# The last tile of a graph layer in four column groups, and the ends of its last two tiles between the next layer's first steps

## The chip, the cores and the metric

The kernel runs on one core of a Trainium2 chip. A time is the device time of one execution in microseconds (us). Three runs of the kernel before gave 1924.24, 1925.73 and 1928.12 us, with a median of 1925.73 us. One further execution was profiled, and all views of the profile come from that one.

## What is computed

Four graph layers, each with a residual and a layer norm, over N = 2708 nodes with F = 256 features and a dense float32 adjacency matrix `adj`. The change touches layer 0 and the beginning of layer 1:

```python
# layer 0
x = layernorm(x + adj @ (x * W))
# layer 1: graph attention, 4 heads of 64
h = (x @ W1).reshape(n, 4, 64)
src, dst = einsum('nhd,d->nh', h, a[:64]), einsum('nhd,d->nh', h, a[64:])
e = leaky_relu(src[:, :, None] + dst.T[None, :, :], 0.2)
attn = softmax(where(adj[:, None, :] > 0, e, -9e15), axis=-1)
out = layernorm(einsum('nhm,mhd->nhd', attn, h)) * gamma + beta
x = layernorm(x + out)
# layers 2 and 3 follow; they read adj again
```

## The kernel before

The nodes are cut into NT = 22 tiles of 128 rows; the last one has 2708 - 21 * 128 = 20 rows. `xs[t]` holds the features of tile t and is overwritten layer by layer. `turn` is one wide tile of 22 * 257 columns; `x0e[t]` is its part for tile t, the input features with a column of ones beside them, so that one matmul gives both the aggregate and the row sum of `adj`. Later layers use `turn` again, for blocks of `adj` and for intermediate rows.

**Layer 0** takes a strip of `adj` for each tile (`load_strip`, on SP's queue, two buffers). `strip_matmul` (line 202) sums over 22 chunks: stationary is the chunk's part of the strip (128 by the tile's rows), moving is `x0e[c]` (257 columns). A float32 matmul appears in the trace as two passes, each with its weight load, so a tile has 44. From the same strip `layer0_mask` makes the tile's columns of `mask` on DVE, and `layer0_own` the diagonal on DVE and a test for negative values on ACT. The end of a tile is `layer0_scale` (row sum and product with `w0_b`, reading PSUM) and `layer0_rest`: add the input (line 467), layer norm (bn_stats, bn_aggr, an add on DVE, a power on POOL, line 167, and a normalisation, line 173), then `layer1_projection`. That transposes the tile on PE (line 179), copies it on ACT (line 181), multiplies it by the weights of layer 1 (`pm`, line 410), takes three exponentials on ACT (lines 413 to 416: `rise`, the factor in `hs`, and `fall`), multiplies into `hs[t]` on DVE (line 417), transposes `fall` on PE (`pf`, line 424) and stores it to DRAM through POOL's queue (line 427).

**Layer 1** needs for a step c the tile `hs[c]`, its column of `rise`, a row of `fall` loaded back and broadcast (`fall_b`), and `mask`. It runs over three rounds g of up to eight destination tiles, in each over two pairs of heads q, and in each over the 22 steps c. A step makes two `p` on DVE (line 665, 128 by 1024), which live in four buffers, and then eight matmuls: `heads` (line 647; 64-column groups, two side by side) and `totals` (line 656; 32-column groups, four side by side, all into one PSUM bank `den`). Every second step does totals first. After the matmuls of a step, `step(c)` issues one piece of each piece-wise list of work in `steps`: in rounds 1 and 2 the ends of the tiles of the round before (`layer1_end`, whose row result `o` lies in eight buffers of a pool), in round 0 nothing.

[...] The list of an engine is not quite the order of the Python code. The framework that builds the program moves instructions forward where its own estimate lets it, so that for instance the passes of tile t+1 stand around the projection of tile t on PE, and a reciprocal that is needed only in layer 2 (line 836) stands at the end of layer 0 on DVE. Memory of a closed pool is used again by the next one, tile by tile, with waits where a buffer overlays another: layer 1's pool `l1` lies where layer 0's pool `l0` with the strips was.

Of the kernel before, what the change touches and what calls it, by code (L numbers as in the profile page):

```python
# [9 lines left out]
F32 = mybir.dt.float32  # L10
# [5 lines left out]
ALU = mybir.AluOpType  # L16
AX = mybir.AxisListType
PSUM = bass.MemoryType.PSUM

P = 128  # L20
# [7 lines left out]
def kernel(  # L28
# [24 lines left out]
    nc = tc.nc  # L53
    N, F = x.shape
    NT = -(-N // P)
# [6 lines left out]
    W = GT * P  # L62
    CT = 32
# [17 lines left out]
    def sz(i):  # L81
        return min(P, N - i * P)
# [4 lines left out]
    def bcast(row, n):  # L87
        return bass.AP(tensor=row.tensor, offset=row.offset, ap=[[0, P], [1, n]])
# [13 lines left out]
    def pool(name, bufs=1, **kw):  # L102
        return tc.tile_pool(name=name, bufs=bufs, reuse_waits="tile", **kw)
# [55 lines left out]
    def moments(src, n):  # L159

        bst = small.tile([P, 6], F32, tag="bn_st", name="bn_st")
        nc.vector.bn_stats(bst[:n], src[:n])
        mv = small.tile([P, 2], F32, tag="bn_mv", name="bn_mv", bufs=12)
        nc.vector.bn_aggr(mv[:n], bst[:n])
        rstd = small.tile([P, 1], F32, tag="bn_rs", name="bn_rs", bufs=12)
        nc.vector.tensor_scalar(rstd[:n], mv[:n, 1:2], EPS, None, ALU.add)  # L166
        nc.gpsimd.tensor_tensor(rstd[:n], rstd[:n], neg_half[:n], ALU.pow)  # L167
        return mv[:n, 0:1], rstd[:n]

    def layernorm(dst, src, n):  # L170

        mean, rs = moments(src, n)
        nc.vector.tensor_scalar(dst[:n], src[:n], mean, rs, ALU.subtract, ALU.mult)

    def transposed(ps, pool, src, n, tag):

        pt = ps.tile([P, 4, P], F32, tag="tr", name="tr")
        for f in range(FC):
            nc.tensor.transpose(pt[:, f, :n], src[:n, f * P : (f + 1) * P], ident[:n, :n])
        dst = pool.tile([P, FC, P], F32, tag=tag, name=tag)  # L180
        nc.scalar.copy(dst[:, :, :n], pt[:, :FC, :n])
        return dst
# [18 lines left out]
    def strip_matmul(acc, s, n, rhs):  # L201
        for c in range(NT):
            nc.tensor.matmul(acc, s[:, c, :n], rhs(c), start=(c == 0), stop=(c == NT - 1))  # L203
# [181 lines left out]
    if True:  # L385
# [13 lines left out]
        if True:  # L399
# [5 lines left out]
            def layer1_projection(pool, t):  # L405
                n = sz(t)
                xt = transposed(ps_t, pool, xs[t], n, "xt")
                pm = ps_t.tile([P, 4, P], F32, tag="tr", name="pm").rearrange("p i q -> p (i q)")
                for f in range(FC):
                    nc.tensor.matmul(  # L410
                        pm[:n, : F + 2 * H], xt[:, f, :n], w1_a[:, f], start=(f == 0), stop=(f == FC - 1)
                    )
# [3 lines left out]
                nc.scalar.activation(fall[:n], pm[:n, :H], AF.Exp, scale=ALPHA - 1.0)  # L416
                nc.vector.tensor_tensor(
                    hs[t][:n, :, :HD],
                    pm[:n, H : H + F].rearrange("p (h d) -> p h d", d=HD),
                    hs[t][:n, :, HD:].to_broadcast([n, H, HD]),  # L420
                    ALU.mult,
                )
                pf = ps_t.tile([P, 4, P], F32, tag="tr", name="pf")
                nc.tensor.transpose(pf[:H, 0, :n], fall[:n], ident[:n, :n])
                turned = pool.tile([H, P], F32, tag="turned", name="turned")
                nc.scalar.copy(turned[:, :n], pf[:H, 0, :n])
                nc.gpsimd.dma_start(fall_d[:, t * P : t * P + n], turned[:, :n])

                for g in [g for g, (lo, hi) in enumerate(spans[:4]) if hi == t + 1]:
                    load_fall(falls[g // 2], g, nc.gpsimd)  # L430

            with pool("l0", 2) as l0:
                w0_b = l0.tile([P, F], F32, name="w0_b", bufs=1)
                nc.scalar.dma_start(w0_b, bcast(w0, F))

                def layer0_mask(t, s, lo=0, hi=NT):
                    n = sz(t)
# [19 lines left out]
                def layer0_scale(t, acc):  # L457
                    n = sz(t)

                    nc.vector.tensor_scalar(rdeg[:n, t : t + 1], acc[:n, F:FE], 1.0, None, ALU.add)  # L460
                    nc.vector.tensor_tensor(xs[t][:n], acc[:n, :F], w0_b[:n], ALU.mult)

                def layer0_rest(t, acc=None):
                    n = sz(t)
                    if acc is not None:
                        layer0_scale(t, acc)
                    nc.vector.tensor_tensor(xs[t][:n], xs[t][:n], x0[t][:n], ALU.add)
                    layernorm(xs[t], xs[t], n)
                    layer1_projection(l0, t)


                ahead = 3
                with pool("prep", side="right") as prep:
# [45 lines left out]
                    acc = ps_acc.tile([P, 512], F32, tag="acc", name="acc")  # L519
                    strip_matmul(acc[:, :FE], strips[ahead], P, lambda c: x0e[c])  # L520
                    for t in range(ahead):
                        layer0_rest(t)
# [25 lines left out]
                falls = [fallp.tile([P, H, 2 * W], F32, tag="fall_b", name="fall_b") for _ in range(2)]  # L548
                nc.sync.dma_start(gamma_b, bcast(gamma, F))
                nc.sync.dma_start(beta_b, bcast(beta, F))  # L550
                for t in range(ahead + 1, NT):
                    s = load_strip(l0, t)
                    last, acc = acc, ps_acc.tile([P, 512], F32, tag="acc", name="acc")
                    strip_matmul(acc[: sz(t), :FE], s, sz(t), lambda c: x0e[c])
                    layer0_mask(t, s)
                    layer0_own(t, s)

                    layer0_rest(t - 1, last)
                layer0_rest(NT - 1, acc)

            l1 = keep_stack.enter_context(pool("l1", 2))
            if True:

                def layer1_end(pool, t, s, sums, dens):
# [12 lines left out]
                    if s == 0:  # L577
                        nc.vector.reciprocal(rden[:n], totals)
                    else:
                        for q in range(H // 2):  # L580
                            nc.vector.reciprocal(rden[:n, q], totals[:, q ^ s])
                    o = pool.tile([P, F], F32, tag="o", name="o", bufs=len(ended))
                    nc.vector.tensor_tensor(
                        o[:n].rearrange("p (h d) -> p h d", d=HD),
                        pt[:n, : H // 2, :].rearrange("p q (i d) -> p (q i) d", d=HD),
                        rden[:n].rearrange("p q i -> p (q i)")[:, :, None].to_broadcast([n, H, HD]),
                        ALU.mult,
                    )
# [26 lines left out]
                for g in range(0, len(spans), 2):  # L615
# [4 lines left out]
                        for i in range(len(segs)):  # L620
                            load_fall(falls[-1], g + i, nc.sync)
                    cols = [(lo * P - at, width(lo, hi)) for lo, hi in segs]
                    sums, steps, halves = [], [], []

                    def step(c):
                        for s in list(steps):
# [13 lines left out]
                    for q in range(H // 2):  # L640
# [42 lines left out]
                    ended = [(t, s, sums, dens) for s, (lo, hi) in enumerate(segs) for t in range(lo, hi)]  # L683


                acc_stack.close()
# [785 lines left out]
```

## Time and profile before

| what | us |
|---|---|
| median of three runs | 1925.73 (1924.24 to 1928.12) |
| the profiled execution's own time | 1929.04 |
| span from its first to its last instruction | 1927.3 |
| layer 0, to the last pass of the 20-row tile | to 255.2 |
| first matmul of layer 1 | 263.92 |
| last matmul of layer 1 | 629.7 |

Times in the views are microseconds from the start of the span. PE is the matmul engine, PEld its weight loads, DVE, ACT and POOL are the vector, scalar and general engines, SP issues loads. A line of a timeline has the start, the length, the engine, the source line, the operation, what it writes and reads with shapes, how many instructions are merged, and in brackets how long the engine had been idle before it and what ended that wait. [...] In a window, each engine's busy time stands before the number of its instructions in brackets, and the granted clock of PE is 1.00 at full speed.

### The profile page before, as it was taken

How to read it: one execution, taken by the hardware profiler on the slowest of the kernel's cores; microseconds unless marked ns; L12 is line 12 of the kernel's file. 1: busy time of each engine (PE TensorE's matmuls, PEld its weight loads, DVE VectorE, ACT ScalarE, POOL GpSimd, SP SyncE). 2: the span in 40 equal slices, each digit the busy share in tenths (PEclk: the TensorE clock that was granted, in tenths of full speed). 3: DMA queues.
4: the chain of work that ended last, by engine and by line, in shares of the span. 5: the costliest groups of instructions: out<-in, count | busy, mean ns of one | idle time of the engine just before them, and what ended most of it. 6: DMA issues, size and time to landing. Idle time of an engine off the chain costs nothing.

```text
span 1927.3 us, 22585 instructions
## 1 busy us (share of the span) xinstructions
PE 1864.0 (97%) x7475; PEld 1011.5 (52%) x7479; DVE 1316.4 (68%) x2409; ACT 617.2 (32%) x1064; POOL 261.2 (14%) x435
## 2 busy tenths in 40 slices
PE   8999989999999999999899999999999999999996
PEld 7788832222233778678444444444445555654444
DVE  4334368899898947455557889585877758855665
ACT  4444400000100103111355656455555555311001
POOL 1212110001112421000001000020200101211101
PEclk9999999999999999999999999999999999999998
DMA  8334400000000647555746656454554444643653
GB/s 294 123 143 159 155 23 1 2 28 9 15 1 23 157 103 194 141 131 121 206 137 187 182 163 174 121 158 112 148 155 127 116 114 124 186 115 97 197 152 101
DMA packets 432922, 235.90 MB, mean 122 GB/s; under 512 B 172150, under 2 KB 420620, under 8 KB 430364
## 3 DMA queue, kind: packets, MB, share of 16 engines
q1 hardware_dynamic: 416158, 207.40, 39.2%
q0 software_dynamic: 7760, 21.20, 3.5%
q10 hardware_dynamic: 8878, 5.76, 1.0%
q8 instruction: 62, 1.02, 0.2%
q14 instruction: 64, 0.52, 0.1%
HBM read 221.61 MB, written 12.65 MB: 122 GB/s over the span
## 4 chain that ended last, share of the span: by engine, by line
PE 80%; DMA 6%; DVE 6%; ACT 3%; issue 2%; SPq 2%; POOL 1%; ACTq 0%; DVEq 0%; POOLq 0%
PE m L309 38%; PE acc L647 10%; PE acc L203 7%; PE bank L1007 7%; PE den L656 5%; PE gate L882 4%; PE bank L983 3%; DMA strip<-in_adj_t_dram 2%; DVE p L665 2%; PE bank L1058 2%; SPq L256 1%; ACT below L452 1%; DVE p L1141 1%; PE pm L410 1%; POOL bn_rs L167 1%
## 5 line engine op out<-in xcount | busy, mean ns | idle before, releaser
L665 DVE SCALAR_TENSOR_TENSOR p<-fall_b,rise,mask 128x1024 f32<-128x1024 f32 (+1 forms) x264 | 297.7, 1150 | 27.1 <-PE den L656 14.6
L1137 ACT ACTIVATE p<-st,e_neg 128x1024 f32<-128x1024 f32 (+1 forms) x198 | 197.1, 1040 | 207.8 <-PE m L309 195.4
L309 PE MATMUL m<-s,xq 128*128 128x512 f32 (+3 forms) x660 | 230.3, 467 | 0.0
L647 PE MATMUL acc<-p,h 128*64 128x512 f32 (+2 forms) x1056 | 224.0, 556 | 3.0 <-DVE p L665 2.8
L203 PE MATMUL acc<-turn,strip 128*128 128x257 f32 (+1 forms) x836 | 191.6, 380 | 0.0
L309 PE MATMUL m<-p,xq 128*128 128x512 f32 (+1 forms) x396 | 183.9, 546 | 0.3 <-DVE p L297 0.3
L1140 ACT ACTIVATE p<-p 128x1024 f32<-128x1024 f32 (+1 forms) x198 | 178.8, 943 | 0.2
L309 PE MATMUL m<-p,x 128*128 128x512 f32 (+1 forms) x396 | 169.7, 547 | 5.1 <-DVE p L1141 4.8
L1141 DVE TENSOR_TENSOR p<-p,blk 128x1024 f32<-128x1024 f32 (+1 forms) x132 | 142.5, 1098 | 42.3 <-ACT p L1140 29.9
L296 DVE TENSOR_TENSOR s<-p 128x512 f32<-128x512 f32 (+1 forms) x132 | 83.1, 631 | 120.9 <-PE m L309 101.9
L203 PEld LDWEIGHTS acc<-turn,strip 128*128 128x128 f32 (+1 forms) x836 | 151.5, 185 | 25.3 <-issue 0.5
L309 PEld LDWEIGHTS m<-s,xq 128*128 128x128 f32 x660 | 124.7, 191 | 75.2 <-issue 58.9
L647 PEld LDWEIGHTS acc<-p,h 128*64 128x64 f32 x1056 | 65.5, 136 | 147.8 <-issue 117.5
L167 POOL TENSOR_TENSOR bn_rs<-bn_rs,neg_half 128x1 f32<-128x1 f32 (+1 forms) x110 | 81.8, 745 | 380.1 <-DVE bn_rs L166 373.2
L309 PE MATMUL m<-s,x 128*128 128x512 f32 (+3 forms) x330 | 127.2, 467 | 0.0
L656 PE MATMUL den<-p,h 128*32 128x512 f32 (+2 forms) x1056 | 124.1, 551 | 2.8 <-DVE p L665 2.7
L309 PEld LDWEIGHTS m<-p,x 128*128 128x128 f32 x396 | 74.9, 191 | 79.2 <-issue 61.1
L309 PEld LDWEIGHTS m<-p,xq 128*128 128x128 f32 x396 | 74.5, 190 | 77.8 <-issue 61.2
L452 ACT ACTIVATE below<-strip 128x384 bf16<-128x384 f32 x132 | 78.5, 594 | 72.6 <-DMA strip<-in_adj_t_dram 69.2
L1141 DVE TENSOR_TENSOR p<-p,turn 128x1024 f32<-128x1024 f32 (+1 forms) x66 | 71.6, 1107 | 21.4 <-ACT p L1140 13.3
L681 ACT COPY den<-den 64x512 f32<-64x512 f32 (+2 forms) x12 | 6.3, 529 | 249.2 <-PE den L656 249.1
L297 DVE TENSOR_TENSOR p<-p 128x512 f32<-128x512 f32 (+1 forms) x132 | 83.0, 629 | 1.7
(243 smaller groups left out, 2514.9 us busy)
## 6 DMA issues: line engine op xcount, KB each, us to landing
strip<-in_adj_t_dram SPq DMA_DIRECT2D x19, 1408.0 KB, 6.2
blk<-in_adj_t_dram SPq DMA_DIRECT2D x88, 256.0 KB, 3.4
blk<-in_adj_t_dram SPq DMA_DIRECT2D x88, 192.0 KB, 4.0
pa<-in_adj_t_dram SPq DMA_DIRECT2D x110, 128.0 KB, 2.7
turn<-in_adj_t_dram SPq DMA_DIRECT2D x44, 256.0 KB, 3.1
blk<-in_adj_t_dram SPq DMA_DIRECT2D x88, 128.0 KB, 2.5
p<-in_adj_t_dram SPq DMA_DIRECT2D x44, 256.0 KB, 3.5
turn<-in_adj_t_dram SPq DMA_DIRECT2D x44, 192.0 KB, 3.2
```

What stands on the lines that cost most here:

```text
L167: nc.gpsimd.tensor_tensor(rstd[:n], rstd[:n], neg_half[:n], ALU.pow)
L203: nc.tensor.matmul(acc, s[:, c, :n], rhs(c), start=(c == 0), stop=(c == NT - 1))
L296: nc.vector.tensor_tensor(s1, a21, a22, ALU.add)
L309: nc.tensor.matmul(dst[:, :w], lt, rt, start=start and not (one_bank and i), stop=stop and not (one_bank and i in (1, 2, 5)))
L452: nc.scalar.activation(below[:, : (hi - lo) * P], s[:, lo:hi].rearrange("p c n -> p (c n)"), AF.Relu, scale=-1.0, accum_out=negative[:, BE ...
L647: nc.tensor.matmul(acc[s][i * HD : (i + 1) * HD, :ws], hs[c][:, 2 * q + i, :HD], ps[i][:, p0 : p0 + ws], **flags,)
L656: nc.tensor.matmul(den[j : j + CT, :ws], hs[c][:, 2 * q + i, HD + 1 - CT :], ps[i][:, p0 : p0 + ws], **flags,)
L665: nc.vector.scalar_tensor_tensor(p[:, :w], falls[g // 2][:, 2 * q + i, :w], rise[:, c, 2 * q + i : 2 * q + i + 1], mask[:, c, at : at + w] ...
L1007: nc.tensor.matmul(g[:, :w], lt, rt, start=(q == 0), stop=(q == len(terms) - 1))
L1137: nc.scalar.activation(p[:, :, :w], st_k[:, :, :w], AF.Relu, scale=-1.0, bias=e_neg[:, at, k : k + 1])
L1140: nc.scalar.activation(p[:, :, :w], p[:, :, :w], AF.Exp, scale=-1.0)
L1141: nc.vector.tensor_tensor(p[:, :, :w], p[:, :, :w], blk[:, i, :, :w], ALU.mult)
```

## The change

Four things are edited.

First, the last tile, of 20 rows, no longer goes through `strip_matmul`. Chunk c goes to the 32-column group c % 4 of the array, with 32 columns of the strip (the 12 beyond the 20 rows are zero padding in `adj_t`), and to the 32 rows of the PSUM tile that belong to it. The four partial sums are copied by ACT to `parts`, and one more float32 matmul with `quarter`, four 32-row identities below each other, adds them (`layer0_last`, tile `pq`).

Second, `layer0_rest` and `layer1_projection` become generators that yield in four places, and the ends of the last two tiles (20 and 21) are not run in layer 0. They are chained into `rest`, with `layer0_last` between them, and stand in `steps` of layer 1's round 0, pair q = 0: one piece after each of the first ten steps. All other tiles are run to the end with `finish`, as before. For tile 20, `layer0_scale` stays in layer 0, ahead of the last strip's mask and diagonal.

Third, `w0_b` and `quarter` live in the pool `keep`, since layer 1 now reads them; the buffers of tiles 20's and 21's ends come from `l1`.

Fourth, `o` of `layer1_end` is no longer a pool tile: it lies in `turn`, in columns `at_row * 256` on, where `at_row` is the tile's place in its round (0 to 7).

```diff
@@ layer1_projection
                 xt = transposed(ps_t, pool, xs[t], n, "xt")
+                yield
                 pm = ps_t.tile([P, 4, P], F32, tag="tr", name="pm").rearrange("p i q -> p (i q)")
...
                     ALU.mult,
                 )
+                yield
                 pf = ps_t.tile([P, 4, P], F32, tag="tr", name="pf")
...
+            w0_b = keep.tile([P, F], F32, name="w0_b")
+            nc.scalar.dma_start(w0_b, bcast(w0, F))
+            quarter = keep.tile([P, CT], F32, name="quarter")
+            nc.vector.tensor_reduce(quarter, ident.rearrange("p (j i) -> p i j", i=CT), AX.X, ALU.add)
...
-                def layer0_rest(t, acc=None):
+                def layer0_rest(pool, t):
                     n = sz(t)
-                    if acc is not None:
-                        layer0_scale(t, acc)
                     nc.vector.tensor_tensor(xs[t][:n], xs[t][:n], x0[t][:n], ALU.add)
-                    layernorm(xs[t], xs[t], n)
-                    layer1_projection(l0, t)
+                    mean, rs = moments(xs[t], n)
+                    yield
+                    nc.vector.tensor_scalar(xs[t][:n], xs[t][:n], mean, rs, ALU.subtract, ALU.mult)
+                    yield
+                    yield from layer1_projection(pool, t)
+
+                def finish(steps):
+                    for _ in steps:
+                        pass
+
+                def layer0_last(t, parts):
+                    pq = ps_t.tile([P, 4, P], F32, tag="tr", name="pq").rearrange("p i q -> p (i q)")
+                    nc.tensor.matmul(pq[: sz(t), :FE], quarter[:, : sz(t)], parts[:, :FE], start=True, stop=True)
+                    layer0_scale(t, pq)
+                    yield
...
-                for t in range(ahead + 1, NT):
+                for t in range(ahead + 1, NT - 1):
...
-                    layer0_rest(t - 1, last)
-                layer0_rest(NT - 1, acc)
+                    layer0_scale(t - 1, last)
+                    finish(layer0_rest(l0, t - 1))
+                t = NT - 1
+                s = load_strip(l0, t)
+                last, acc = acc, ps_acc.tile([P, 512], F32, tag="acc", name="acc")
+                if sz(t) <= CT:
+                    for c in range(NT):
+                        j = c % TILES * CT
+                        nc.tensor.matmul(
+                            acc[j : j + CT, :FE], s[:, c, :CT], x0e[c], start=(c < TILES), stop=(c >= NT - TILES)
+                        )
...
+                layer0_scale(t - 1, last)
+                layer0_mask(t, s)
+                layer0_own(t, s)
+                if sz(t) <= CT:
+                    parts = keepr.tile([P, W], F32, tag="sum00", name="parts0")
+                    nc.scalar.copy(parts[:, :FE], acc[:, :FE])
...
             l1 = keep_stack.enter_context(pool("l1", 2))
+            rest = [layer0_rest(l1, NT - 2), layer0_rest(l1, NT - 1)]
+            if sz(NT - 1) <= CT:
+                rest.insert(1, layer0_last(NT - 1, parts))
...
-                    o = pool.tile([P, F], F32, tag="o", name="o", bufs=len(ended))
+                    o = turn[:, at_row * F : (at_row + 1) * F]
...
-                    sums, steps, halves = [], [], []
+                    sums, steps, halves = [], [itertools.chain(*rest)] if g == 0 else [], []
```

More of the change, by code (lines that the diff above doesn't have):

```diff
@@ L430, in layer1_projection @@
                     load_fall(falls[g // 2], g, nc.gpsimd)
+            w0_b = keep.tile([P, F], F32, name="w0_b")
+            nc.scalar.dma_start(w0_b, bcast(w0, F))
+            quarter = keep.tile([P, CT], F32, name="quarter")
+            nc.vector.tensor_reduce(quarter, ident.rearrange("p (j i) -> p i j", i=CT), AX.X, ALU.add)
             with pool("l0", 2) as l0:
-                w0_b = l0.tile([P, F], F32, name="w0_b", bufs=1)
-                nc.scalar.dma_start(w0_b, bcast(w0, F))
                 def layer0_mask(t, s, lo=0, hi=NT):
@@ L521 @@
                     for t in range(ahead):
-                        layer0_rest(t)
+                        finish(layer0_rest(l0, t))
                     nw = weights(prep, "nw", neigh_w)
@@ L556, with layer1_end @@
                     layer0_own(t, s)
-                    layer0_rest(t - 1, last)
-                layer0_rest(NT - 1, acc)
+                    layer0_scale(t - 1, last)
[9 more added lines that the diff above has]
+                        )
+                else:
+                    strip_matmul(acc[: sz(t), :FE], s, sz(t), lambda c: x0e[c])
+                layer0_scale(t - 1, last)
[4 more added lines that the diff above has]
+                    nc.scalar.copy(parts[:, :FE], acc[:, :FE])
+                else:
+                    layer0_scale(t, acc)
             l1 = keep_stack.enter_context(pool("l1", 2))
+            rest = [layer0_rest(l1, NT - 2), layer0_rest(l1, NT - 1)]
+            if sz(NT - 1) <= CT:
+                rest.insert(1, layer0_last(NT - 1, parts))
             if True:
-                def layer1_end(pool, t, s, sums, dens):
+                def layer1_end(pool, t, s, sums, dens, at_row):
                     n = sz(t)
@@ L682 @@
                         sums.append(got)
-                    ended = [(t, s, sums, dens) for s, (lo, hi) in enumerate(segs) for t in range(lo, hi)]
+                    ended = [(t, s, sums, dens, t - segs[0][0]) for s, (lo, hi) in enumerate(segs) for t in range(lo, hi)]
                 acc_stack.close()
```

## The prediction

> **What bounds the kernel now.** I began with the page: PE is busy 97% of the span, and the chain of waits runs over PE for 80% of it. So a change pays only where it takes matmul time away or fills a hole in PE. Which holes lie at the place of the change I asked of the timeline of PE and of DVE, the windows around it, and the line groups for the rates.
>
> ```profile
> span 1927.3 us, 22585 instructions
> PE 1864.0 (97%) x7475; PEld 1011.5 (52%) x7479; DVE 1316.4 (68%) x2409; ACT 617.2 (32%) x1064; POOL 261.2 (14%) x435
> ...
> PE 80%; DMA 6%; DVE 6%; ACT 3%; issue 2%; SPq 2%; POOL 1%; ACTq 0%; DVEq 0%; POOLq 0%
> ```
>
> The timeline of PE where layer 0 ends (start, length, engine, line, what, count, idle time before it and its releaser):
>
> ```profile
> 246.81 8.43 PE L203 MATMUL acc<-turn,strip 128*20 128x257 f32 x38
> 255.17 0.44 PE L179 MATMUL tr<-ident,x 128*128 128x128 f32 x2
> 256.07 1.16 PE L410 MATMUL pm<-w_a,xt 128*128 128x264 f32 x4 [0.46 <-ACT xt L181]
> 257.62 0.27 PE L424 MATMUL pf<-ident,fall 128*4 128x128 f32 x1 [0.40 <-ACT fall L416]
> 258.72 0.29 PE L179 MATMUL tr<-ident,x 20*128 20x20 f32 x2 [0.82 <-DVE x L173]
> 259.35 1.31 PE L410 MATMUL pm<-w_a,xt 128*20 128x264 f32 x4 [0.34 <-ACT xt L181]
> 261.08 0.19 PE L424 MATMUL pf<-ident,fall 20*4 20x20 f32 x1 [0.42 <-ACT fall L416]
> 263.92 3.38 PE L647 MATMUL acc<-p,h 128*64 128x512 f32 x8 [2.65 <-DVE p L665]
> 267.23 1.92 PE L656 MATMUL den<-p,h 128*32 128x512 f32 x16
> 269.08 3.74 PE L647 MATMUL acc<-p,h 128*64 128x512 f32 x16
> ```
>
> See two things. The tile of 20 rows spends a full tile's time: 38 of its 44 passes take 8.43 us, 0.217 us a pass from start to start in the chain of waits (8.26/38 for the tile before), as for tiles of 128 rows. Then the ends of tiles 20 and 21 run as one chain through PE, ACT, DVE and POOL, and layer 1's first matmul waits until 263.92 for two `p` that stand behind that chain on DVE:
>
> ```profile
> 247.11 0.42 DVE L417 TENSOR_TENSOR h<-pm,h 128x256 f32<-128x256 f32 x1
> 255.28 0.15 DVE L460 TENSOR_SCALAR rdeg<-acc 20x1 f32<-20x1 f32 x1 [7.75 <-PE acc L203]
> ...
> 261.06 0.41 DVE L417 TENSOR_TENSOR h<-pm,h 20x256 f32<-20x256 f32 x1 [2.40 <-ACT fall L416]
> 261.40 4.85 DVE L665 SCALAR_TENSOR_TENSOR p<-fall_b,rise,mask 128x1024 f32<-128x1024 f32 x4
> 268.34 2.48 DVE L665 SCALAR_TENSOR_TENSOR p<-fall_b,rise,mask 128x1024 f32<-128x1024 f32 x2 [2.09 <-PE den L656]
> ```
>
> DVE idles 7.75 us before the end of the 20-row tile. The windows show the rest (PE busy, PEld, DVE, ACT, POOL, then granted clock):
>
> ```profile
> 255.24:263.92 8.68, 3.59 (x14) 1.48 (x15) 5.82 (x13) 1.56 (x10) 3.07 (x5) 0.78 0.35 96
> 263.92:267.30 3.38, 3.38 (x12) 0.83 (x16) 2.34 (x2) 0.00 (x0) 0.00 (x0) 0.57 0.01 2
> 267.30:278.30 11.00, 11.00 (x68) 2.65 (x69) 9.17 (x8) 0.00 (x0) 0.00 (x0) 1.00 0.00 0
> ```
>
> In 8.68 us PE works 3.59, and the hole drops its clock, so that layer 1's first heads run at half speed. After 267.3 a pair of steps takes 5.52 us (3.67 heads and 1.85 totals in the chain of waits): 2.76 a step, PE-bound, with DVE 2.48 busy.
>
> [...] the 32-column totals take 1.85/16 = 0.116 us a pass, the 64-column heads, two at a time, 0.229, hence about 0.459 alone. Heads and totals alternate with no visible hole[...]. [...] half-microsecond windows show it at half from 260.0 to 266.9[...]. [...]
>
> **The change part by part**, against the profiled execution (1929.04 us around a span of 1927.3; the median of the three runs is 1925.73, 3.31 lower; I take the difference to both).
>
> *The tile of 20 rows.* Its 44 passes of 257 columns go round four column groups. At the rate of the totals a pass takes 0.116*257/512 = 0.058 us: 2.6 us instead of 44*0.217 = 9.6. Bounds: 0.054 a pass (0.217/4) gives 2.4; with no overlap 9.6. The fastest stream of load and matmul pairs in the trace, the 32-column logit matmuls (132 in 8.43 us in the chain), has 0.064: 2.8. I take 2.6, a gain of 7.0. Beside these passes stand, unchanged, the projection and turning of tile 19.
>
> *When layer 1 can start.* In the built program's order DVE goes straight from tile 19's `h` (ends 247.53) into four `p`, whose inputs are long there; the second also waits for the last pass of the 20-row tile, whose strip its buffer overlays. On PE: tile 19's transposes from 243.69; with fewer passes ahead of it pm(19) runs about 244.6 to 245.7 and pf(19) ends about 246.3; then 34 passes, 2.0, to 248.35. After them PE does tile 20: transposes 0.38, ACT copies `parts` (257 columns, estimated at 0.40 from `xt`'s 0.36 for 256) and then `xt`, pm 1.1, ACT's three exponentials to about 250.65, pf 0.2, and the added pq, two passes of 0.217. The first heads can issue at about 251.35. Both `p` are ready at about 250.0, so PE's own queue is late next. Before, they began at 263.92, but at half clock: 3.38 for 1.83, so their full-speed start was 267.30 - 1.83 = 265.47. Gain to here 14.1 if the clock holds.
>
> *What is paid back.* Tile 21's PE work moves into steps 7 to 9: 0.29 + 1.0 + 0.2 = 1.5. On DVE a `p` may start only when PE has finished the step two back, and takes 2.48 of 2.76, so DVE has 0.28 a step spare, and more behind the first four `p`, where it waits for PE from 252.4 to 254.15. Laid out step by step with the order of the built program: `h` of tile 20 (0.42) and scale (0.15 + 0.40) fall into that wait, free. The add of 0.81 and the reciprocal of 0.27 stand ahead of step 4's `p`: PE waits 0.6. Statistics of 0.42 + 0.17 + 0.14 ahead of step 6: 0.3. The normalisation of 0.40 ahead of step 7: 0.1. `h` of tile 21 (0.41) stands between step 10's two `p`, where pm's 1.0 has given slack: free. The reciprocal root on POOL (0.56) lies beside two `p`. Sum 1.0. If no slack counted, the DVE pieces after the start (0.81 + 0.27 + 0.73 + 0.40 + 0.41) would cost 2.6.
>
> *Queues and other buffers.* SP's six loads into `turn` wait for x0 of tile 21, whose add moves to about 260; before, they ran at 253.15 to 260.4. Behind them SP has nothing until 383.99, and the data are read at 766: free, and some 120 us would be needed to cost. On POOL, tile 20's store of `fall` stands in the same place; the last store follows step 9, at about 282, read after 384. `o` in `turn` uses columns below 2048, the loads those from 3606: no wait is added, and the first loads of layer 2 wait for layer 1's last `p` and matmul as before (629.85). `quarter` costs DVE about 0.2 at 14 us, where PE waits for strips. w0_b only changes its pool. All at zero; nothing later is reordered on PE.
>
> **Sum:** 14.1 - 1.5 - 1.0 = 11.6. Profiled execution 1929.04 - 11.6 = 1917.4; median 1925.73 - 11.6 = 1914.1.
>
> **The rivals.**
> - *The clock still drops.* The thin stretch from 248.35 to 251.35 has PE at some 2.1 busy of 3.0. [...] One half-clock window costs 1.7: gain 9.9, 1915.8.
> - *The first steps are DVE-bound.* Every piece delays PE in full, and `parts` or pq takes another 0.5: gain 11.6 - 1.6 - 0.5 = 9.5, 1916.2. For it: DVE is at 90% in these steps. Against it: the wait of 2.09 behind the first four `p` in the trace.
> - *The column groups do not overlap,* because each pass has another moving tensor: the 7.0 is lost, gain 4.6, 1921.1. Against it: the totals also alternate two `p` and two segments. With weight loads exposed too (0.108 each), 44 passes take 14.3, 4.7 over before: 1925.8, no change.
> - *Slower: stalls keep the clock down.* [...] PE runs those 28 us at half clock. Eight windows at 1.7 cost 13.7, from seven on the gain is used up: 1927.8. For it: the start at half clock now. Against it: the largest stall that I find is 0.6 in 3.4 us[...].
>
> **How the numbers follow.** My forecast 0.72; clock drops once 0.11; DVE-bound 0.08; no overlap 0.05, of which 0.03 would not be told from no change; slower 0.03; 0.01 for a gain past 14. The forecast's own bounds are a gain of 10.5 to 13.0, from the passes at 2.4 to 2.8, pauses of ACT at 0.5 either way, and the half-clock windows of other places (two more in this trace, from 635.5 and from 935.9, 1.7 each way[...]). With the first two rivals inside, and 2 us for the spread of the three runs, 1910.0 to 1919.0. A measurement of this kernel tells 0.2%, 3.9 us, from no change: faster (below 1921.9) 0.94, same 0.03, slower 0.03.
>
> **What would show it.** Right: the 20-row tile's passes about 0.06 apart; four `p` on DVE right after tile 19's `h`; the first heads near 251 and at full clock; step 9's matmuls ending some 11 to 12 us earlier than now; everything from 384 on shifted by that. Wrong: passes 0.2 apart, half clock in the first steps, waits of PE for `p` of over 0.6 in steps 2 to 9, or a gain at 300 us that is given back near 630.

## The result, and the profile after

Five runs of the changed kernel gave a median of 1913.02 us (1912.09 to 1913.24), five of the kernel before, on the same chip, 1925.85 (1924.24 to 1928.12). The ratio is 0.9931, with a 95% interval of 0.9921 to 0.9942: by it the change takes 13.3 us off, between 11.2 and 15.2. The profiled execution of the changed kernel took 1913.03 us around a span of 1911.2.

The page of the changed kernel: its head, and the first line of its chain of waits.

```profile
span 1911.2 us, 22590 instructions
PE 1855.2 (97%) x7477; PEld 1011.0 (53%) x7481; DVE 1318.3 (69%) x2410; ACT 617.6 (32%) x1065; POOL 265.5 (14%) x435
...
PE 81%; DVE 7%; DMA 5%; ACT 3%; issue 2%; SPq 1%; POOL 1%; ACTq 0%; DVEq 0%; POOLq 0%
```

The kernel is bound as before. PE's busy time falls by 8.8 us of a span that falls by 16.1, so about half of the difference is matmul time (the first heads' return to full speed is part of it), and half is holes. Where both lie, the timeline of PE shows:

```profile
242.34 0.38 PE L179 MATMUL tr<-ident,x 128*128 128x128 f32 x2
242.65 0.64 PE L581 MATMUL acc<-turn,strip 128*32 128x257 f32 x6
243.21 1.16 PE L411 MATMUL pm<-w_a,xt 128*128 128x264 f32 x4
244.30 0.63 PE L581 MATMUL acc<-turn,strip 128*32 128x257 f32 x4
244.86 0.27 PE L426 MATMUL pf<-ident,fall 128*4 128x128 f32 x1
245.06 2.35 PE L581 MATMUL acc<-turn,strip 128*32 128x257 f32 x34
247.34 0.44 PE L179 MATMUL tr<-ident,x 128*128 128x128 f32 x2
248.29 1.16 PE L411 MATMUL pm<-w_a,xt 128*128 128x264 f32 x4 [0.50 <-ACT xt L181]
249.84 0.27 PE L426 MATMUL pf<-ident,fall 128*4 128x128 f32 x1 [0.40 <-ACT fall L417]
250.04 0.61 PE L483 MATMUL pq<-parts,quarter 128*20 128x257 f32 x2
250.58 1.94 PE L684 MATMUL acc<-p,h 128*64 128x512 f32 x8
...
265.35 4.01 PE L684 MATMUL acc<-p,h 128*64 128x512 f32 x16
```

A pass of 257 columns is drawn 0.38 long (median of line 203 in the kernel before), while in a stream the next one starts 0.217 after it, so the rate of a stream is about its length divided by its count. Where 38 passes took 8.43 in one piece, 34 now take 2.35, and ten stand in two pieces ahead of them. After them stand only two waits, 0.50 and 0.40, before layer 1's first heads. Those start at 250.58, right behind pq, with no bracket: PE waits for nobody there. They take 1.94 where they took 3.38, and the granted clock is 1.00 for 0.57, so they run at full clock. The windows (length, then busy time of PE, PEld, DVE, ACT and POOL, granted clock, DMA share, GB/s) from tile 20's last pass to the first heads, from there to the first totals, and from there to layer 1's last matmul:

```profile
242.50:250.58 8.08, 7.18 (x61) 3.28 (x58) 7.07 (x12) 2.24 (x11) 3.29 (x4) 1.00 0.24 67
250.58:252.45 1.87, 1.87 (x10) 0.48 (x9) 1.75 (x4) 0.00 (x0) 0.53 (x1) 1.00 0.15 31
252.45:616.49 364.04, 357.30 (x2258) 104.79 (x2256) 329.28 (x454) 21.08 (x60) 43.80 (x60) 1.00 0.04 12
```

The same three of the kernel before; the middle one ends at 267.30 here, while the first totals start at 267.23:

```profile
243.86:263.92 20.06, 14.97 (x65) 6.43 (x64) 8.58 (x21) 2.50 (x15) 4.92 (x8) 0.90 0.19 54
263.92:267.30 3.38, 3.38 (x12) 0.83 (x16) 2.34 (x2) 0.00 (x0) 0.00 (x0) 0.57 0.01 2
267.23:629.70 362.47, 355.83 (x2251) 103.79 (x2249) 327.42 (x447) 20.46 (x55) 40.19 (x57) 1.00 0.04 10
```

The account of the stretch follows. From tile 20's last pass to the first totals it was 267.23 - 243.86 = 23.37, and is 252.45 - 242.50 = 9.95: a gain of 13.42. The rest of layer 1 grew from 362.47 to 364.04, which pays 1.57 back. The stretch as a whole went from 385.84 to 373.99, a gain of 11.85. The forecast had 11.6.

The two spans differ by about 4.2 more than that. Of this, 1.36 had come before tile 20's last pass (243.86 against 242.50), 1.18 lies between layer 1's last matmul and layer 2's first (4.48 against 3.30), and 1.6 after it. Apart from the new places of `w0_b`, `quarter` and `o`, which places only tries below, the change touches none of the three, and all three scatter over the kernels below: the first point lies between 241.95 and 244.02; the border is 4.56 in one of them and 3.30 in most; what follows it takes 1289.4 to 1293.6. The stretch scatters least (385.84 and 386.48 in the two kernels that have the old path, 373.99 to 374.12 in four that have the new one), so it is what I compare below. It also fits the medians: 11.85 lies inside the interval of 11.2 to 15.2.

### The profile page after: what moved, and what is told of

The parts are those of the page before. It is cut to its first block, busy times and chain, and to the rows that moved or that the text cites. A ratio compares the mean times of both kernels' runs of the same rounds, so it can differ in the third digit from the quotient of the medians.

```text
span 1911.2 us, 22590 instructions
## 1 busy us (share of the span) xinstructions
PE 1855.2 (97%) x7477; PEld 1011.0 (53%) x7481; DVE 1318.3 (69%) x2410; ACT 617.6 (32%) x1065; POOL 265.5 (14%) x435
## 3 DMA queue, kind: packets, MB, share of 16 engines
q8 instruction: 62, 1.02, 0.2%
## 4 chain that ended last, share of the span: by engine, by line
PE 81%; DVE 7%; DMA 5%; ACT 3%; issue 2%; SPq 1%; POOL 1%; ACTq 0%; DVEq 0%; POOLq 0%
PE m L309 38%; PE acc L684 10%; PE acc L203 7%; PE bank L1044 7%; PE den L693 5%; PE gate L919 4%; PE bank L1020 3%; DVE p L702 2%; PE bank L1095 2%; DMA strip<-in_adj_t_dram 1%; ACT below L457 1%; DVE p L1178 1%; SPq L256 1%; PE pm L411 1%; POOL bn_rs L167 1%
## 5 line engine op out<-in xcount | busy, mean ns | idle before, releaser
L203 PE MATMUL acc<-turn,strip 128*128 128x257 f32 x792 | 181.5, 380 | 0.0
L203 PEld LDWEIGHTS acc<-turn,strip 128*128 128x128 f32 x792 | 147.5, 190 | 20.1
L299 DVE TENSOR_TENSOR s<-p,s 128x512 f32<-128x512 f32 (+1 forms) x132 | 83.4, 632 | 2.0
```

## The experiments

My theory was the forecast's: the passes overlap in four groups (about 6), the heads start early at full clock because tile 21's chain is no longer ahead of them, and some 2 are paid back. The rivals were that one part brings it all, that the 32-column form as such is faster, that the new places of `o` and `w0_b` matter, and that the clock makes the difference. The table has what the runs gave. "To heads" is from tile 20's last pass to layer 1's first heads, the stretch runs on to layer 1's last matmul. The last column is the ratio to the kernel before in the same series, with its 95% interval; where it is missing, the kernel was run once.

| kernel | to heads | stretch | median us (runs) | ratio |
|---|---|---|---|---|
| before | 20.06 | 385.84 | 1925.85 (5) | |
| changed | 8.08 | 373.99 | 1913.02 (5) | 0.9931 (0.9921 to 0.9942) |
| groups only | 16.91 | 383.79 | 1922.75 (9) | 0.9979 (0.9969 to 0.9989) |
| moved only | 14.03 | 379.95 | 1920.74 (5) | 0.9966 (0.9952 to 0.9979) |
| places only | 19.83 | 386.48 | 1927.23 (13) | 1.0000 (0.9992 to 1.0009) |
| before, hole filled | 19.83 | 384.15 | 1923.68 (11) | 0.9982 (0.9973 to 0.9991) |
| one group | 14.05 | 379.98 | 1920.51 (6) | 0.9963 (0.9950 to 0.9975) |
| groups in turn | 12.06 | 377.99 | 1917.91 (4) | 0.9948 (0.9932 to 0.9963) |
| groups by two | 8.53 | 374.49 | 1914.07 (1) | |
| parts late | 8.09 | 374.00 | 1914.38 (1) | |
| early blocks | 8.10 | 374.12 | 1912.59 (5) | 0.9925 (0.9912 to 0.9939) |
| no beta | 8.08 | 374.02 | 1911.77 (1) | |

The kernel before had a median of 1926.93 (27 runs) beside the four kernels from groups only to hole filled, of 1928.04 (9) beside one group and groups by two, and of 1927.36 (9) beside the others. The series ran on different chips, so medians are compared within a series.

### One part at a time

*Groups only*: the 20-row tile goes round the groups, but both ends are finished in layer 0.

```diff
+                finish(layer0_rest(l0, t - 1))
+                finish(layer0_last(t, parts))
+                finish(layer0_rest(l0, t))
...
-            rest = [layer0_rest(l1, NT - 2), layer0_rest(l1, NT - 1)]
...
-                    sums, steps, halves = [], [itertools.chain(*rest)] if g == 0 else [], []
+                    sums, steps, halves = [], [], []
```

> Column groups as in the change, but both tiles' ends run to their end in layer 0. Theory (the gain is two separate parts): the 44 passes take 3.0 us (0.068 each, as after shows) for 9.6, 6.6 less; the copy to parts (0.37) and pq (0.6) come into tile 21's serial chain: 5.4 us faster than before (4.5 to 6.5), median about 1920.4; the hole in PE stays, so the first heads of layer 1 run at half clock again. Rival A (the tile's passes were hidden behind the wait that follows, and all of the gain comes from the moved ends): within 1 us of before.

*Moved only*: the ends go into layer 1, but the tile takes 44 passes in a row.

```diff
-                        j = c % TILES * CT
-                        nc.tensor.matmul(
-                            acc[j : j + CT, :FE], s[:, c, :CT], x0e[c], start=(c < TILES), stop=(c >= NT - TILES)
-                        )
+                strip_matmul(acc[: sz(t), :FE], s, sz(t), lambda c: x0e[c])
...
-                    layer0_scale(t, pq)
+                    layer0_scale(t, acc)
```

> Tile 21 goes through full-width passes as before; the ends of tiles 20 and 21 stand between layer 1's steps. Theory: the last pass ends as before, tile 20's transposes, pm and pf follow in about 2.9 us, then the first heads at full clock: 7.3 us earlier than before in full-speed terms, of which 1.6 are paid back in steps 4 to 9: 5.7 us faster (4.5 to 7.0), median about 1920.1. Sum of this and the groups alone near 11 us. Rival A: the whole 12.8 us. Rival B (the moved ends only pay because the short tile leaves DVE early): under 2 us.

*Places only*: the kernel before with `w0_b` and `quarter` in `keep`, and `o` in `turn`.

```diff
-                    o = pool.tile([P, F], F32, tag="o", name="o", bufs=len(ended))
+                    o = turn[:, at_row * F : (at_row + 1) * F]
```

> Only the places change: o in turn, w0_b and quarter in the kept pool. Theory: no wait is touched, within 1 us of before (1925.9). Rival C (some us of the gain come from the o buffers gone from the pools at the border of layers 1 and 2): 1 us or more faster, and the first matmul of layer 2 earlier against the last one of layer 1 (before: 4.4 us after it).

Moved only gained 5.89 in the stretch and 6.2 in the median, near what was expected of it. Places only is nothing, between 0.9992 and 1.0009. Groups only is the miss: 2.05 in the stretch. Its median gained 4.2 (2.1 to 6.0 by the ratio), which doesn't rule out the 5.4 expected, so the reading rests on the trace. The passes are as short as in the changed kernel, so the saving must be lost behind them. Its timeline of PE from pq on:

```profile
249.63 0.61 PE L483 MATMUL pq<-parts,quarter 128*20 128x257 f32 x2
253.34 0.27 PE L179 MATMUL tr<-ident,x 20*128 20x20 f32 x2 [3.11 <-DVE x L473]
253.95 1.83 PE L411 MATMUL pm<-w_a,xt 128*20 128x264 f32 x4 [0.34 <-ACT xt L181]
256.20 0.19 PE L426 MATMUL pf<-ident,fall 20*4 20x20 f32 x1 [0.42 <-ACT fall L417]
259.04 3.68 PE L682 MATMUL acc<-p,h 128*64 128x512 f32 x8 [2.65 <-DVE p L700]
```

pq stands behind tile 20's pm and pf in PE's list and runs 2.6 us after the last pass (247.04). Before, DVE could scale tile 21 0.04 after it, straight from PSUM. So tile 21's whole chain comes later by that and by pq itself, and PE waits 3.11 for it at the transposes: they start 6.30 after the last pass, for 3.48 in the kernel before (0.5 is won back at DVE's add, which takes 0.35 for 0.81). The windows say the same: the hole from the last pass to the heads, and the heads:

```profile
247.04:259.04 12.00, 4.63 (x18) 1.72 (x17) 5.36 (x13) 1.93 (x11) 3.08 (x5) 0.79 0.32 88
259.04:262.65 3.61, 3.61 (x8) 0.77 (x9) 2.34 (x2) 0.00 (x0) 0.00 (x0) 0.50 0.01 2
```

The hole is 12.00, against 8.68 before: 3.3 of the passes' 6.5 are gone, 2.8 of them by the later chain and 0.5 by tile 21's pm, which runs at half clock (1.83 for 1.31). Half clock lasted 10.24 us instead of 6.83 and reached into the totals, so that 0.8 more are lost there and 0.3 in the heads. The two parts alone sum to 2.05 + 5.89 = 7.94 in the stretch; together they give 11.85. The other 3.9 belong to neither. Some 2.3 of them are the chain: the groups' saving reaches the heads in full only if tile 21's chain, which the groups lengthen by pq, doesn't stand before them. The other 1.6 are the longer half clock, and how much of it a kernel pays depends in part on where it falls, as the next section shows. The medians don't settle this remainder: the gains of 4.0, 6.5 and 13.3 by the ratios are each uncertain by 2 to 3.

That it then reaches them in full shows in moved only, where PE has the same list with the long form in it:

```profile
245.24 8.44 PE L203 MATMUL acc<-turn,strip 128*20 128x257 f32 x38
253.61 0.44 PE L179 MATMUL tr<-ident,x 128*128 128x128 f32 x2
...
256.31 1.94 PE L670 MATMUL acc<-p,h 128*64 128x512 f32 x8
```

From here to the changed kernel the heads move by 14.03 - 8.08 = 5.95; the passes save 6.5 and pq costs 0.54, which makes 5.96.

### The clock

*Hole filled*: the kernel before, with matmuls of zeros into an unused PSUM bank, 18 in all (bfloat16, 512 columns), between the pieces of the last two tiles' ends.

```diff
+    def fill(i, k):
+        if fills:
+            with tc.issue_after(i.ins):
+                for _ in range(k):
+                    nc.tensor.matmul(fills[0], zeros, zeros[:, :1].to_broadcast([P, 512]), start=True, stop=True)
...
+        fill(i, 1)
...
+                fill(i, 1)
...
+                fill(i, 3 if t < NT - 1 else 11)
```

> The kernel before, with 20 bf16 passes of zeros into an unused PSUM bank put between the ends of tiles 20 and 21, so that PE is busy in the hole; nothing else changes. Theory (the hole drops the clock, and that is 1.5 us of the gain): granted clock 1.00 through the first heads, their 8 passes take 1.9 us for 3.4, tile 21's pm 1.1 for 1.3: about 1.6 us faster less up to 0.6 for passes that stand in the way, so 1.0 to 1.7. Rival D (the slow first heads are not a matter of PE's idleness): heads still take 3.4, and the time is not lower than before.

Its windows of the same hole and heads:

```profile
255.34:263.85 8.51, 7.42 (x32) 3.11 (x32) 5.82 (x13) 1.56 (x10) 3.07 (x5) 1.00 0.38 101
263.85:265.72 1.87, 1.87 (x9) 0.49 (x9) 1.87 (x2) 0.00 (x0) 0.00 (x0) 1.00 0.01 4
```

PE is busy 7.42 of 8.51 and the clock stays at 1.00. The heads start hardly earlier against the last pass of tile 20 (19.83 for 20.06, and 19.83 in places only too), but take 1.87. The stretch gains 1.69, and the median 3.3 (1.7 to 5.2). So the clock is worth about 1.7 of the change's 11.85; the hole itself is the larger part. The price isn't fixed. In places only, which has the path of the kernel before, the half clock also lasts 6.83 us but begins at 261.25 instead of 260.03; its heads take 3.68 and its totals 2.52 (for 1.92), and against it hole filled gains 2.33.

The shortest stretch at half clock in the trace of the kernel before lasts 3.41 us (635.50 to 638.91); 6.83 is two of these. How busy PE was in the 3.41 us just before the clock fell: 1.85 in the kernel before (256.62 to 260.03), 1.54 in places only, 0.43 in groups only. In the changed kernel the thinnest 3.41 us of this place hold 2.51 (246.81 to 250.22), and the clock stays. No busy time that decides is shown: elsewhere in the changed kernel 3.41 us with 1.68 busy come right before half clock (618.86 to 622.27), and 3.41 us with 1.68 busy (1892.03 to 1895.44) have 1.00 behind them for another 3.41.

### What makes the passes overlap

*One group*: moved only, with 32 columns of the strip for 20, all in group 0. *Groups in turn*: the changed kernel, with all chunks of group 0 first, then those of group 1, and so on. *Groups by two*: two chunks of a group at a time.

```diff
-                strip_matmul(acc[: sz(t), :FE], s, sz(t), lambda c: x0e[c])
+                strip_matmul(acc[:CT, :FE], s, CT, lambda c: x0e[c])
```

> The kernel with only the ends moved, but the last tile's matmuls take 32 columns of the strip for 20 and so run in the array's 32-column form, all in its first column group. Theory (a pass in one column group is as slow as a full one, 0.217 us; chunks sorted by group took 0.154 only because PE lets the next group's passes start while up to four of the former group's still wait): 9.6 us for the tile, within 1 us of the kernel with only the ends moved (1920.7). Rival H (the 32-column form is itself faster): 0.154 a pass, 6.8 us for the tile, 2.8 us faster.

```diff
-                    for c in range(NT):
+                    for c in sorted(range(NT), key=lambda c: c % TILES):
```

> The changed kernel, but the 22 chunks come sorted by group: all of group 0, then all of group 1, and so on, so that neighbours in PE's order share a column group. Same matmuls, same sums. Theory (passes overlap only with neighbours in another group[...]): the passes are about 0.2 us apart again instead of 0.068, the tile takes 9 to 9.6 us for 3.0, and the time is 6 to 6.6 us above the changed kernel, about 1919.5. Rival F (the gain of the groups comes from fewer columns of weights or output per matmul, in whatever order): within 1 us of the changed kernel.

```diff
-                    for c in range(NT):
+                    for c in sorted(range(NT), key=lambda c: (c // (2 * TILES), c % TILES)):
```

> The changed kernel with the chunks in runs of two to a group (four passes), then the next group. Theory with up to four passes of look-ahead: about two groups work at a time, the 44 passes take 4.0 to 5.5 us. Strict order (only the last pass of a run overlaps with the next group): about 7 us. If groups were independent of order: 3.0 us.

One line each from the timeline of PE, first one group, then groups in turn, then the two lines of groups by two:

```profile
244.92 8.45 PE L203 MATMUL acc<-turn,strip 128*32 128x257 f32 x38
```

```profile
246.27 5.91 PE L581 MATMUL acc<-turn,strip 128*32 128x257 f32 x38
```

```profile
245.22 1.08 PE L581 MATMUL acc<-turn,strip 128*32 128x257 f32 x14
246.44 1.93 PE L581 MATMUL acc<-turn,strip 128*32 128x257 f32 x26
```

One group takes 8.45 for 38 passes, as with 20 columns (8.44 in moved only), and its median, 1920.51, is that of moved only: the 32-column form by itself brings nothing. In turn I had expected no overlap, and was wrong. Counted up to the start of tile 20's transposes, a pass takes 0.154, between one group's 0.221 and the changed kernel's 0.067. The starts of single passes in the trace show why. They are in us; the first two lines are the part around the border from group 0 to group 1, the third is from the changed kernel.

```
groups in turn, group 0: 246.267 246.508 246.725 246.942 247.158 247.375
groups in turn, group 1:                 246.731 246.972 247.188 247.405 247.622 ...
changed: 245.061 245.067 245.074 245.081 | 245.301 245.308 245.314 245.321 | 245.517 ...
```

Within a group a pass starts 0.217 after the one before. But group 1's first starts at 246.731, while three passes of group 0, which stand before it in PE's list, have not started. The same at the other two borders. In the changed kernel the order of the list is both passes of a chunk, then the next chunk in the next group; four groups start within 0.020, and each round of four costs one pass's 0.217. In runs of two chunks, four passes, four groups still start together: the first piece of 14 starts as 4, 4, 3 and 3, which are runs of four in three groups and a single chunk in the fourth. The heads come only 0.45 later. So PE lets passes of another group go ahead of a few waiting ones: three at these borders, where the expectations took up to four, an estimate. Runs of four passes in one group cost little and runs of ten or twelve cost 4 us; nothing between was run. The group's number of a pass isn't in the record; I assigned the starts by their counts, six left in group 0 and twelve in group 1, which fit no other way that I found. Nor does the trace show a pass's place in PE's list: that the list has the order of the program here is taken from the code, and that the framework had moved passes is not excluded.

### What stands before the heads, and behind layer 1

*Parts late*: ACT's copy of the partial sums is held behind the copy to `xt`. *No beta*: leaves out layer 1's addition of `beta` on POOL (line 610), which the framework places beside layer 0's ends. *Early blocks*: layer 2's first two blocks of `adj` go into free columns of `turn`, and so are loaded before layer 1 ends.

```diff
-                    parts = keepr.tile([P, W], F32, tag="sum00", name="parts0")
-                    nc.scalar.copy(parts[:, :FE], acc[:, :FE])
...
+                    with tc.issue_after(copies[-1].ins):
+                        nc.scalar.copy(parts[:, :FE], acc[:, :FE])
```

> The changed kernel, but ACT copies tile 20's transposed rows to xt before it copies the partial sums to parts. Theory (the hole of 0.5 us ahead of tile 20's pm is ACT's copy to parts): pm starts 0.4 us earlier against tile 20's transposes, and the first heads too, about 2.8 us after the transposes begin instead of 3.24. Rival: pq then waits for parts and gives it back.

```diff
-                    nc.gpsimd.tensor_tensor(xs[t][:n], xs[t][:n], beta_b[:n], ALU.add)
```

> The changed kernel without POOL's addition of beta to the rows of x in layer 1 (that addition is left out; beta is all zeros in these inputs). Theory (POOL's two-operand additions and DVE's two-operand operations [...]slow each other): the addition of the input in layer 0 on DVE takes 0.41 us for 0.75, the first four p 4.9 us for 5.5, the pair beside the later addition 2.5 for 2.95; the time falls by less than 1 us, since PE sets the pace there. Rival: the durations stay, because the 0.75 comes from reading a row that was just written.

```diff
-            pa = pool.tile([P, 2, 2, w], F32, tag="pa", name="pa", bufs=5)
+            if r == 0 and c < 2:
+                end = NT * FE - 4 * W - c * 4 * w
+                pa = turn[:, end - 4 * w : end].rearrange("p (m h w) -> p m h w", m=2, h=2)
+            else:
+                pa = pool.tile([P, 2, 2, w], F32, tag="pa", name="pa", bufs=5)
```

> The changed kernel, and the first two blocks of adj for layer 2 go to columns of turn that are free in layer 1 instead of to buffers over layer 1's p, so that they are loaded before layer 1 ends. Theory (the same kind of hole as the one that the change closed: PE waits 3.3 us between the last matmul of layer 1 and the first of layer 2 for a load that can only be issued when p is free, and then runs a window at half clock): hole below 1 us, 2.3 to 4.0 us faster than the changed kernel, about 1910. Rival G (the ends of layer 1's last tiles hold that border anyway): hole of 2 us or more, within 1 us of the changed kernel.

Parts late changed nothing: pm still starts 0.51 after the transposes. In the changed kernel's timeline of ACT one sees that the copy costs nobody anything, as it runs while PE transposes (247.34 to 247.78), and `xt` follows at once:

```profile
247.45 0.37 ACT L591 COPY parts<-acc 128x257 f32<-128x257 f32 x1 [2.03 <-PE acc L581]
247.86 0.37 ACT L181 COPY xt<-tr 128x256 f32<-128x256 f32 x1
```

No beta left the stretch as it was (374.02), but shows a cost that the forecast had priced wrongly. The line of the add of the input, all 22 instructions (shortest, median and longest in ns), in the changed kernel and then in no beta:

```profile
L470 DVE TENSOR_TENSOR x<-x,turn x22: 405/752/757, 39.1 to 258.7; 128x256 f32<-128x256 f32 x21, 20x256 f32<-20x256 f32 x1
```

```profile
L470 DVE TENSOR_TENSOR x<-x,turn x22: 407/425/428, 38.7 to 259.2; 128x256 f32<-128x256 f32 x21, 20x256 f32<-20x256 f32 x1
```

Beside POOL's addition DVE's takes 0.75; without it 0.42. In the changed kernel the first four tiles' adds, before POOL's first addition, take 0.41 to 0.42 too, and so does tile 21's (0.41), at 258.67 ahead of layer 1's step 4, where POOL does nothing. So POOL's addition costs DVE's 0.33.

Early blocks cut the border between layers 1 and 2 from 3.30 to 1.26, which is neither below 1 nor above 2, and the median stayed (1912.59; its ratio's interval covers the changed kernel's). Its timeline of PE and the window of 620 to 640 show where it went:

```profile
618.67 0.92 PE L309 MATMUL m<-turn,x 128*128 128x226 f32 x4
...
631.87 0.62 PE L309 MATMUL m<-pa,x 128*128 128x226 f32 x2 [1.02 <-DMA pa<-in_adj_t_dram]
```

```profile
620.00:640.00 20.00, 18.45 (x105) 16.24 (x104) 19.41 (x83) 1.60 (x6) 9.67 (x14) 1.00 0.71 178
```

PE starts sooner and then waits 1.02 for a later block. Its 18.45 busy of these 20 us can't be set beside the changed kernel's 19.17, since that one ran at half clock for 3.4 of them (0.91). The starts of layer 2's matmuls, counted from layer 1's last, can: the first comes 2.04 earlier than in the changed kernel, the 101st only 0.9. By this reading the stream of blocks, which starts only when layer 1's buffers come free, holds that stretch, and two blocks in hand move the wait and don't remove it. None of the kernels is clearly faster than the changed one.

## Why the prediction was right

- **The passes.** Forecast 2.6 us, a gain of 7.0. In the chain of waits they take 0.56, 0.56 and 2.30, together 3.42, where they took 0.98, 0.54 and 8.38, together 9.90: a gain of 6.5. The term was 0.5 too large because it used a stream's rate for pieces. Rounds of four cost 0.217 each, and tile 19's pm and pf cut the stream: 6 passes are two rounds, 4 are two, 34 are ten. Fourteen rounds are 3.04, eleven would be 2.4; the rest is 0.13 at the head of each piece. Inside a round the overlap is nearly whole: four passes start within 0.020.
- **The change of form** between passes was priced at nothing, because the lines show no hole there. The lines hide it behind the drawn ends of the passes (0.39 for pm's last, 0.40 for the first behind it); the starts of single passes show a price. From pm to tile 20's full-width passes the starts lie 0.223 apart (to 233.41), from pm to the column-group passes 0.316 (to 244.30). Rounds of heads or of totals lie 0.41 to 0.47 apart, and 0.52 where one follows the other. So a change of form costs about 0.1; what in the change takes it, no run tells. The kernel before has the same gap (0.316, to 246.06), so in the forecast's sum it cancels, except for the one more that is in pq's 0.54. The price was wrong, and it did no harm.
- **The start.** Forecast to gain 14.1; 13.42 came, and the passes' 0.5 is most of the difference. The reason held: both `p` were done at 248.74 (by their single records), 1.8 before the heads, and PE's own list, with pq last, was late.
- **The clock.** The windows have 1.00 throughout. The thinnest 3.41 us have PE busy 2.51, 74%, where those before the drop in the kernel before have 1.85, 54%. Hole filled puts the price of the drop at 1.7. That is the rival's figure only by chance: the rival's was an estimate, 3.41 us at half clock, as from 635.50 in the kernel before, with PE busy throughout, and this drop lasted 6.83, with PE idle in much of its first half.
- **Paid back.** Forecast 1.5 on PE and 1.0 on DVE, together 2.5; measured 1.57. PE's part is 1.22: transposes 0.23, pm 0.88, pf 0.11. DVE's is a single stall of about 0.27, between the heads of steps 5 and 6 (counted from 0), whose line of 16 takes 4.01 for 3.74. The statistics stand ahead of step 6's `p`, and the forecast had them at 0.3; the normalisation ahead of step 7, at 0.1, shows no stall. The remaining 0.1 I can't place. The 0.6 at step 4 failed: it had the add at 0.81, taken from a tile where POOL adds beside it, and here it took 0.41, which accounts for 0.4 of the 0.6.

The timeline of DVE has step 4's add, and two more places that the forecast didn't have:

```profile
246.09 5.52 DVE L702 SCALAR_TENSOR_TENSOR p<-fall_b,rise,mask 128x1024 f32<-128x1024 f32 x4
...
258.67 0.41 DVE L470 TENSOR_TENSOR x<-x,turn 20x256 f32<-20x256 f32 x1
259.00 0.27 DVE L873 RECIPROCAL rdeg<-rdeg 128x22 f32<-128x22 f32 x1
...
273.11 2.95 DVE L702 SCALAR_TENSOR_TENSOR p<-fall_b,rise,mask 128x1024 f32<-128x1024 f32 x2 [0.23 <-PE acc L684]
```

The first four `p` take 5.52, not 4.85, and the pair at 273.11 2.95, not 2.48. Both have an addition of POOL beside them, which alone takes 0.72, in the timeline of POOL:

```profile
247.88 1.45 POOL L610 TENSOR_TENSOR x<-x,beta_b 128x256 f32<-128x256 f32 x1 [1.60 <-PE tr L179]
...
273.39 1.58 POOL L610 TENSOR_TENSOR x<-x,beta_b 20x256 f32<-20x256 f32 x1 [6.79 <-PE tr L179]
```

Neither is on the path: the first two `p` are early enough (the third has most of the loss, 1.76 for 1.27), and at 273 PE has tile 21's own work. In no beta, where both additions are gone, that third `p` takes 1.28 and the pair 2.48, and the stretch is 374.02. So of the terms that add up to 11.6, the start was 0.7 too high and what is paid back 0.9 too high, and the errors cancelled.

- **Queues, buffers, places** at zero: places only confirms it as a whole (within 0.1% either way). That no load or store became late was read from the order, and not tried singly.
- **The rivals.** No overlap fell with one group and groups in turn, DVE-bound steps with the timeline above, and the slow one with the granted clock of 1.00 after 252.45 and the largest stall of 0.27. The two parts weren't priced singly in the forecast; when they were, for the first experiments, groups only was over-rated because the list of PE around pq was not laid out.

What stays open: why the border was 4.48 in the profiled execution of the kernel before and 3.30 in most others. One group had the long one too (4.56), and it has the moved ends, which other kernels with 3.30 have as well; so it doesn't go with the change, and I didn't try it.

## What to carry to other kernels

A short last tile can be spread over column groups, and then a round of four passes costs the time of one (0.217 here). Count rounds between the interruptions, not a mean rate, add the change of form at each interruption (about 0.1 here), and keep runs in one group short (runs of four passes cost 0.45 more here, runs of ten or twelve 4). Ask where a saved microsecond goes: a chain that starts from the end of the saved work keeps only what its own added link and the engine's order leave, and here what reached the heads nearly doubled (3.15 to 5.95) once the chain was taken from before the next stage's first matmul. When an instruction moves to another place, take its duration from what will run beside it there, and not from where it stood (the same add took 0.75 beside POOL's addition and 0.41 without).

## What was unexpected of the hardware

- Matmuls of another column group start before waiting ones of the group before: three were still waiting at each border of groups in turn. I had expected them to start in order; in this trace they don't, if PE's list has the order of the code.
- A change between full-width passes, 64-column heads, 32-column totals and column-group passes costs about 0.1 from start to start (0.316 for 0.223 behind pm), and the lines of the timeline don't show it.
- DVE and POOL hold each other up where these operations overlap: DVE's add goes from 0.42 to 0.75, four `p` from 4.85 to 5.52, POOL's addition from 0.72 to 1.45 and 1.58, and its power of a single column from 0.56 to 1.47 (at 265.12, beside `p`). The order of the starts matters. Where POOL's addition starts 0.25 before DVE's add, it keeps its 0.72 and the add is long; where it starts during a `p`, that `p` keeps its 1.28, the addition is long, and so is the `p` after it.
- Half clock after the hole lasted 6.83 us in the kernel before and 10.24 in groups only, two and three times 3.41. In the kernel before it began with PE busy 1.85 of the 3.41 us before.
